# Float32 matmuls for the third batch's projection, and a start whose engine orders are written out as lists, in an attention and feed-forward block of 16 batches

## The chip, the cores and the metric

The kernel runs on 1 core of one Trainium2 chip. The metric is the device time of the whole kernel in microseconds (us), as the median of several runs. Five engines work side by side, each through its own list of instructions in order: PE (TensorE; its weight loads are shown apart as PEld), DVE (VectorE), ACT (ScalarE), POOL (GpSimd) and SP (SyncE, which here only issues DMAs). They wait for one another through semaphores. Matmul results stand in PSUM, eight banks of 128 x 512 float32; everything else stands in SBUF.

## The reference, cut to what matters

`x` is 16 x 512 x 512 (batch, row, column), `ctx` 16 x 512 x 1024. `_layernorm` has no weights.

```python
    def _hnet_depool(h, h_patch_full, patch_lens):
        ...
        _, s = jax.lax.associative_scan(comb, (a_b, u), axis=1)
        depool = s.reshape(bsz, plen, D_MODEL)
        plug = jnp.clip(jnp.cumsum(boundary_mask, axis=1) - 1, 0, plen - 1)
        depool_out = depool[jnp.arange(bsz)[:, None], plug]
        return depool_out + h
    h = rmsnorm(embeds, g_res)
    h = jnp.einsum('bld,ed->ble', h, W_in) + b_in
    h_patch = rmsnorm(patch_embeds, g_init)
    return _hnet_depool(h, h_patch, patch_lens)
...
        r = jax.nn.sigmoid(jnp.einsum('btc,dc->btd', xr, W_r))
        k = jnp.einsum('btc,dc->btd', xk, W_k)
        k_act = jnp.square(jax.nn.relu(k))
        out = r * jnp.einsum('btc,dc->btd', k_act, W_v)
...
    x = x + _L0_xattn_ref(_layernorm(x, axis=-1), ctx_2048, mask_BxS2_if0, ...)
    x = x + _L0_ffn_ref(_layernorm(x, axis=-1), ...)
```

Here `xr` and `xk` mix a row with the row before it (weights `mu_r`, `mu_k`). For each batch there are four products of 512 x 512 by 512 x 512: a (with `W_in`), k, r and v.

## The kernel before

**A batch.** Each batch is cut into four groups j of 128 rows, and the 512 columns into four chunks c. The names in the profile, with their lines:

- `x`: the batch, loaded, later the sum, later the output. Batches 0 to 2 (`BY_PE`, line 420) are transposed by PE into four PSUM banks `tx` (`turn_x`, 629); the others are loaded transposed.
- `split_x` (642): ACT copies each `tx` chunk to a rounded high half `xh[:,0]`, and DVE writes the low half `xh[:,1]` = `tx` - high.
- `wsa` is `W_in` in float32, scaled by `g_res` and less a mean that four float32 matmuls form in the bank `pm` (1112 to 1130); `wha` and `wla` are its halves (`hi_w` 578, `lo_w` 582). The other weights are split likewise: `whk`, `wlk` and so on.
- `a_mm` (786), and `a_first` (799) for batch 0: the projection into the bank `pa`, with three passes for each j (high by high, high by low, low by high; `QW`, 600), each of four matmuls. `a_end` (813) on DVE adds `pa`, times the row's scale `rs`, to `x`, which frees the bank.
- `cx`: the context; ACT squares it, DVE scans it (`scan_u` 733, `scan` 748), with a carry between the rows by PE in the bank `pc`. SP writes the result to DRAM as `dr`; POOL fetches rows of it by index (`gather`, 820; the indices are `plug`) and adds them to `x`.
- `norm2` (827): statistics on DVE, a power on POOL, and `y` on DVE (for batches 0 to 3); PE transposes `y` into four banks `tr` (852). `mix` (864): ACT `prev` and DVE `both` write `pv`, which is split into `m`. Each batch has four mixes for k and four for r.
- k (bank `pk`), r (`pr`) and v (`pw`) are three-pass products like a. The first of batch 0, `k_first` (895), needs four banks.
- `plugs` (1021): counts of boundaries by PE into `cp`; DVE turns them to running marks (`marks`), PE sums those over the rows, and DVE forms the index `plug` (`index`, 1062).

**What sets the order.** Every step is a piece added with `add` (516): the engines that can do it with an estimated cost, what it reads and writes, and a due time. `Plan.order` (119) plays these through and gives each engine its fixed order. Buffers have kinds with few places (`SLOTS`, 308): `ps` and `tr` are four PSUM banks each, `op` are 16 tiles of 128 x 2 x 512. Where `ORDER` names pieces for an engine, that engine takes these in just that order first; before, `ORDER` is empty (437) and due times, shifted by hand for each stage (`SHIFT`, 326), decide. `warm` (585) puts small matmuls ahead of some pieces. All instructions are recorded by one helper, so their line is L300.

Of the kernel before, what the change touches and what calls it, by code (L numbers as in the profile page):

```python
# [11 lines left out]
F32 = mybir.dt.float32  # L12
# [9 lines left out]
P = 128  # L22
T = 512
D = 512
# [265 lines left out]
class InOrder:  # L290
# [25 lines left out]
    "tr": [P, D],  # L316
}
PASS = 0.935
PERIOD = lambda i: (("a", i + 1), ("k", i))
TAT = {3: (0, 1, 2, 3)}  # L320
TAT_OF = {0: {0: (0, 1, 2, 3)}, 1: {0: (0, 1, 2, 3)}, 2: {0: (0, 1, 2, 3)}, 3: {0: (0, 1), 2: (2, 3)}, 4: {0: (0, 1), 2: (2, 3)}}
AHEAD = 20.0
EASE = 1.0
SKIP = 6.0
# [64 lines left out]
    ("sq", 4): 2.2,  # L389
    ("stat1", 4): 2.5,  # L390
    ("store", 4): -10.4,
    ("plugs", 8): -40.0,
    ("plugs", 12): -40.0,
}
ONLY = {
    ("rv", 0): 0,
# [37 lines left out]
KR_DVE_LATE = ()  # L434
NKR = 4
LATE = ()
ORDER = {}
RAW_IN = {2: ("op", "raw")}
CX_IN = {}
NLATE = 4  # L440
NWHOLE = 2
Y_DVE = (0, 1, 2, 3)
LEAD = 12.0
LEAD_LATE = 15.0
NLEAD = 6
# [10 lines left out]
def block_kernel(  # L456
# [77 lines left out]
    def K(name, *parts):  # L534
        return [(name, p) for p in (parts or (0,))]
# [7 lines left out]
    TR = (("tr",), [P, D], F32)  # L543
    HI = ((ACT, 0.52), (DVE, 0.34)) if HI_DVE else ((ACT, 0.52),)
    LO = ((DVE, 0.61), (POOL, 1.26))

    def copy(e, o, i):
        (e.tensor_copy if e is dve else e.copy)(o, i)
# [26 lines left out]
    def st(k, c):  # L575
        return S[f"ws{k}{c // 2}"][:, c % 2]
# [8 lines left out]
    def warm(key, tiles, due):  # L585

        n = WARM.get(key, 0)
        if not n:
            return tiles

        def fn(e):
            for _ in range(n):
                e.matmul(S[next(iter(tiles))][:, :P], ones, ones, start=True, stop=True)

        add((PE, 0.064 * n), fn, (), K(next(iter(tiles))), new=tiles, due=due - 0.064 * n)
        return None
# [32 lines left out]
    def turn_x(b):  # L629
# [3 lines left out]
        for j in J:  # L633
            def fn(e, j=j):
# [4 lines left out]
                [y for n in ns for y in K(n, j)] + ([] if j else K(f"txa{b}")),  # L639
                new=None if j else new, due=when(j))  # L640

    def split_x(b, c):
        if b in BY_PE:
            n, t = f"xh{b}_{c}", f"tx{b}_{c}"
            add((ACT, 0.52), lambda e: e.copy(S[n][:, 0], S[t]), K(t, *J), K(n, 0), new={n: OP}, early=40)
            add((DVE, 0.6), lambda e: e.tensor_tensor(S[n][:, 1], S[t], S[n][:, 0].bitcast(F32), ALU.subtract),
                K(t, *J) + K(n, 0), K(n, 1))
            return
        n, rn = f"xh{b}_{c}", f"raw{b}_{c // 2}"
        add(HI, lambda e: copy(e, S[n][:, 0], S[rn][:, c % 2]), K(rn), K(n, 0), new={n: OP}, early=40)  # L650
        add(LO, lambda e: e.tensor_tensor(S[n][:, 1], S[rn][:, c % 2], S[n][:, 0].bitcast(F32), ALU.subtract),
            K(rn) + K(n, 0), K(n, 1))
# [95 lines left out]
    def scan(b):  # L748
# [23 lines left out]
        for j in J:  # L772
# [10 lines left out]

            add((SP, 0.5), put, K(n), K(f"dr{b}", j), moves=0.73)

    def a_mm(b, j, due, kind=PS):
        n = f"pa{b}_{j}"
        sl = slice(j * P, (j + 1) * P)
        new = warm(("a", b, j), {n: kind}, due)
        for k, (q, w) in enumerate(QW):  # L790
            def fn(e, k=k, q=q, w=w):
                for c in range(NC):
                    e.matmul(S[n], S[f"xh{b}_{c}"][:, q, sl], W2("a", w)[:, c],
                             start=(k == 0 and c == 0), stop=(k == 2 and c == NC - 1))

            add((PE, PASS), fn, [y for c in range(NC) for y in K(f"xh{b}_{c}", q) + K("wla" if w else "wha", c)],
                K(n), new=None if k else new, due=due + k * PASS, early=AHEAD)

    def a_first():

        ns = [f"pa0_{j}" for j in J]
        new = warm(("a", 0, 0), {n: TRP for n in ns}, due["a", 0, 0])
        for k, (q, w) in enumerate(QW):
            for c in range(NC):
                def fn(e, k=k, q=q, w=w, c=c):
                    for j in J:
                        e.matmul(S[ns[j]], S[f"xh0_{c}"][:, q, j * P : (j + 1) * P], W2("a", w)[:, c],
                                 start=(k == 0 and c == 0), stop=(k == 2 and c == NC - 1))

                add((PE, PASS), fn, K(f"xh0_{c}", q) + K("wla" if w else "wha", c), [K(n)[0] for n in ns],  # L810
                    new=new if k == c == 0 else None, due=due["a", 0, 0] + (4 * k + c) * PASS, early=AHEAD)
# [209 lines left out]
    def plugs(b0, n):  # L1021
        cp = f"cp{b0}"
        cnt = lambda: S[cp][:, : n * NJ].rearrange("p (b j) -> p b j", j=NJ)
        pb = lambda: S[cp][:, n * NJ :]
        for b in range(b0, b0 + n):
            oh = f"oh{b}"
            add((DVE, 0.6),
                lambda e, b=b, oh=oh: e.tensor_tensor(
                    S[oh], hj[:, 0, :, b].unsqueeze(2).broadcast_to([P, NC, P]),
                    iota.unsqueeze(1).broadcast_to([P, NC, P]), ALU.is_equal),  # L1030
                K("hj") + K("msk"), K(oh), new={oh: (("tmp",), [P, NC, P], F16)}, early=25, soft=True)

            def count(e, b=b, oh=oh):
                for c in range(NC):
                    e.matmul(cnt()[:, b - b0], S[oh][:, c], ohj[:, c, b], start=(c == 0), stop=(c == NC - 1))

            add((PE, 0.1), count, K(oh) + K("hj") + (K(cp, "a") if b > b0 else []),
                K(cp, b) + ([] if b > b0 else K(cp, "a")),
                new=None if b > b0 else {cp: (("ps", "tr"), [P, n * (NJ + 1)], F32)})

        def marks_1(e):

            bm = S[f"bm{b0}"] = spool.tile([P, 1, NJ], F16, tag="bm", name=f"bm{b0}")
            run = S[f"run{b0}"] = spool.tile([P, 1, NJ], F32, tag="pf", name=f"run{b0}")
            for j in J:
                if j:
                    e.tensor_scalar(run[:, 0, j : j + 1], cnt()[:, 0, j : j + 1], 1.0, run[:, 0, j - 1 : j], ALU.min, ALU.add)
                else:
                    e.tensor_scalar(run[:, 0, 0:1], cnt()[:, 0, 0:1], 1.0, None, ALU.min)
            e.tensor_copy(bm[:, 0, NJ - 1 : NJ], run[:, 0, NJ - 1 : NJ])  # L1050

        def marks(e):
            bm = S[f"bm{b0}"] = spool.tile([P, n, NJ], F16, tag="bm", name=f"bm{b0}")
            e.tensor_scalar(bm, cnt(), 1.0, None, ALU.min)
            for j in range(1, NJ):
                e.tensor_tensor(bm[:, :, j], bm[:, :, j], bm[:, :, j - 1], ALU.add)

        add((DVE, 0.5 if n == 1 else 0.8), marks_1 if n == 1 else marks, K(cp, *range(b0, b0 + n)), K(f"bm{b0}"), soft=n > 1)
        add((PE, 0.05), lambda e: e.matmul(pb(), tri, S[f"bm{b0}"][:, :, NJ - 1], start=True, stop=True),
            K(f"bm{b0}") + K("tri"), K(cp, "p"))  # L1060

        def index(e):
            pf = spool.tile([P, n, NJ], F32, tag="pf", name=f"pf{b0}")
            e.tensor_tensor(pf, S[f"run{b0}" if n == 1 else f"bm{b0}"], pb().unsqueeze(2).broadcast_to([P, n, NJ]), ALU.add)
            e.tensor_scalar(pf, pf, -1.0, 0.0, ALU.add, ALU.max)
            e.tensor_copy(plug[:, b0 : b0 + n], pf)

        add((DVE, 0.6), index, K(cp, "p"), K("plug", *range(b0, b0 + n)), due=INF if b0 else P_DUE, soft=True)


    due, t = {}, T0
# [1 line left out]
    def slot(key, cost=3 * PASS):  # L1073
        nonlocal t
        due[key] = t
        t += cost

    for what, b in START:
        if b < NB and (what != "x" or b in BY_PE):
            for j in J:  # L1080
                slot((what, b, j), 0.43 if what in "tx" else 3 * PASS)
    for i in range(NB):
        n1 = i + 1 < NB
        for what, b in PERIOD(i):
# [10 lines left out]
        due["end", i] = t  # L1095


    add((SP, 0.5), lambda e: e.dma_start(small_in, small_d), (), K("cols") + K("msk") + K("tri"), moves=0.45, at=-9.5)
    load_w("a", at=-9)
    add((SP, 0.5), lambda e: e.dma_start(consts, consts_d), (), K("consts"), moves=0.4, at=-8.5)  # L1100
    for j in J:
        load_x0(j, -8)
    add((DVE, 0.07), lambda e: e.tensor_scalar(om, mu, -1.0, 1.0, ALU.mult, ALU.add), K("cols"), K("om"))

    def heat(e):
# [26 lines left out]
    for c in range(NC):  # L1132
        lo_w("a", c)

    def row(src, dst, k, at):
        add((SP, 0.5), lambda e: e.dma_start(dst, src.unsqueeze(0).broadcast_to([P, D])), (), K(k), moves=0.8, at=at)

    row(ginit[0:D], g_bc, "g_bc", -6.4)
    for j in J:
        load_ctx(0, j, at=-6)  # L1140
    row(brow, b_bc, "b_bc", -5.9)
    at = {k: 0.2 * i - 5 for i, k in enumerate(LOADS)}
    at.update({f"cx1_{j}": at["cx1"] + 0.01 * j for j in J if "cx1" in at})
    if NB > 1:
# [10 lines left out]
    def prepare_batch(b):  # L1155
# [47 lines left out]
            for j in J:  # L1203
                gather(b, j)
        stage = ("a", b)
        if b == 0:
            a_first()
        for j in J:
            if b:
                a_mm(b, j, due["a", b, j], PST if b == 1 else PS)  # L1210
            a_end(b, j)
        if late:
            stage = ("gather", b)
# [122 lines left out]
```

## Time and profile before

| | |
|---|---|
| median of 3 runs | 809.4 us (808.52 to 810.18) |
| the profiled execution, its time | 808.87 us |
| its span, first to last instruction | 807.1 us |
| mean granted TensorE clock | 0.994 |
| PE idle before an instruction, up to 71.5 us | 10.1 us in 10 waits |
| the same from there to the end | 3.7 us in 7 waits |
| projection of batch 0, first matmul | 18.27 us |
| first k matmul (batch 0) | 70.28 us |
| first gather issued by POOL | 36.28 us |
| DVE busy, 10 to 60 us in steps of 10 | 8.77, 9.14, 8.47, 9.39, 9.90 us |
| DMA share, 0 to 30 us in steps of 10 | 0.80, 1.02, 0.72 |

The span is what the profile covers; the time is measured around it and is 1.8 us longer. In the lists of the profile a group has its engine, operation, the tiles it writes and reads (numbers left out), its count and its times. A wait is the idle time of an engine before an instruction, and is put down to what released it last. PEclk is the clock that TensorE was granted, 1.00 being full. One execution is profiled, so all durations come from that one.

### The profile page before, as it was taken

How to read it: one execution, taken by the hardware profiler on the slowest of the kernel's cores; microseconds unless marked ns; L12 is line 12 of the kernel's file. 1: busy time of each engine (PE TensorE's matmuls, PEld its weight loads, DVE VectorE, ACT ScalarE, POOL GpSimd, SP SyncE). 2: the span in 40 equal slices, each digit the busy share in tenths (PEclk: the TensorE clock that was granted, in tenths of full speed). 3: DMA queues.
4: the chain of work that ended last, by engine and by line, in shares of the span. 5: the costliest groups of instructions: out<-in, count | busy, mean ns of one | idle time of the engine just before them, and what ended most of it. 6: DMA issues, size and time to landing. Idle time of an engine off the chain costs nothing. (4 is left out here: it accounts for less than half of the span.)

```text
span 807.1 us, 11158 instructions
## 1 busy us (share of the span) xinstructions
PE 788.4 (98%) x3627; PEld 628.2 (78%) x3627; DVE 594.3 (74%) x1323; ACT 486.0 (60%) x950; POOL 453.1 (56%) x374
## 2 busy tenths in 40 slices
PE   7998999999999999999999999999999999999997
PEld 4776877878787888888788888878788888888885
DVE  6899798989789696785857679685866949464432
ACT  6937496655483767467566756457675664655540
POOL 2843766574767656567665556537856554661220
PEclk8999999999999999999999999999999999999999
DMA  9867586895775777667665766756786674430011
GB/s 327 270 95 262 104 220 170 288 220 160 144 234 147 179 199 206 157 209 145 212 140 171 220 157 209 157 162 152 184 234 157 209 138 171 73 89 0 9 45 52
DMA packets 52554, 134.69 MB, mean 167 GB/s; under 512 B 4752, under 2 KB 5264, under 8 KB 50576
## 3 DMA queue, kind: packets, MB, share of 16 engines
q1 hardware_dynamic: 35744, 102.39, 37.3%
q0 software_dynamic: 16608, 31.46, 24.2%
q8 instruction: 28, 0.46, 0.2%
q14 instruction: 30, 0.25, 0.1%
q10 hardware_dynamic: 144, 0.13, 0.0%
HBM read 85.73 MB, written 33.55 MB: 148 GB/s over the span
## 5 line engine op out<-in xcount | busy, mean ns | idle before, releaser
L300 POOL TENSOR_TENSOR m<-pv,m 128x512 fp32r<-128x512 f32 x86 | 120.9, 1414 | 121.3 <-ACT m L300 59.7
L300 PE MATMUL pa<-wha,xh 128*128 128x512 f32 x512 | 136.7, 404 | 5.8 <-DVE x L300 2.0
L300 PE MATMUL pw<-whv,ka 128*128 128x512 f32 x512 | 139.0, 398 | 0.0
L300 POOL DMA_INDIRECT x<-dr,plug x64 | 113.2, 1769 | 45.3 <-issue 17.0
L300 PE MATMUL pr<-whr,m 128*128 128x512 f32 x512 | 138.4, 397 | 0.0
L300 PE MATMUL pk<-m,whk 128*128 128x512 f32 x512 | 133.8, 396 | 0.6 <-DVE x L300 0.6
L300 ACT ACTIVATE pv<-tr,om 128x384 f32<-128x384 f32 (+1 forms) x256 | 100.8, 485 | 52.4 <-PE tr L300 28.5
L300 DVE SCALAR_TENSOR_TENSOR pv<-tr,small,pv 128x511 f32<-128x511 f32 x128 | 94.9, 741 | 38.7 <-ACT pv L300 37.9
L300 PEld LDWEIGHTS pa<-wha,xh 128*128 128x128 f32 x512 | 96.9, 191 | 31.9 <-DVE x L300 2.8
L300 PEld LDWEIGHTS pk<-m,whk 128*128 128x128 f32 x512 | 95.6, 188 | 24.8 <-DVE x L300 1.0
L300 PEld LDWEIGHTS pr<-whr,m 128*128 128x128 f32 x512 | 95.5, 188 | 23.0 <-DVE kr L300 0.4
L300 PEld LDWEIGHTS pw<-whv,ka 128*128 128x128 f32 x512 | 95.0, 188 | 21.8
L300 ACT CAST m<-pv 128x512 fp32r<-128x512 f32 x128 | 76.1, 642 | 37.1 <-DVE pv L300 31.8
L300 ACT ACTIVATE sg<-pr 128x512 f32<-128x512 f32 x64 | 38.1, 598 | 95.6 <-PE pr L300 88.6
L300 DVE TENSOR_TENSOR ka<-kr,ka 128x512 fp32r<-128x512 f32 x48 | 35.9, 749 | 76.3 <-ACT ka L300 76.2
L300 DVE TENSOR_TENSOR sg<-pw,sg 128x512 f32<-128x512 f32 (+1 forms) x65 | 43.9, 676 | 41.5 <-PE pw L300 41.5
L300 ACT ACTIVATE junk<-cx 128x1024 bf16<-128x1024 f32 x64 | 67.5, 1055 | 6.7 <-DMA cx<-cx 6.1
L300 PE MATMUL pa<-wla,xh 128*128 128x512 f32 x256 | 71.2, 401 | 0.3 <-POOL wla L300 0.3
L300 ACT ACTIVATE y<-x,r 128x512 f32<-128x512 f32 x48 | 38.9, 814 | 53.7 <-DVE r L300 37.4
L300 PE MATMUL pw<-wlv,ka 128*128 128x512 f32 x256 | 70.4, 397 | 0.0
L300 PE MATMUL pr<-wlr,m 128*128 128x512 f32 x256 | 70.3, 396 | 0.0
L300 PE MATMUL pk<-m,wlk 128*128 128x512 f32 x256 | 69.9, 396 | 0.0
(116 smaller groups left out, 1238.9 us busy)
## 6 DMA issues: line engine op xcount, KB each, us to landing
cx<-cx SPq DMA_DIRECT2D x64, 512.0 KB
dr<-cx SPq DMA_DIRECT2D x64, 256.0 KB
out<-x SPq DMA_DIRECT2D x31, 512.0 KB
x<-x SPq DMA_DIRECT2D x15, 1024.0 KB
x<-bc POOLq DMA_DIRECT2D x14, 1024.0 KB
raw<-xT SPq DMA_DIRECT2D x26, 512.0 KB
wsa<-winT SPq DMA_DIRECT2D x2, 512.0 KB
x<-x SPq DMA_DIRECT2D x4, 256.0 KB
```

Source lines behind the costliest of these rows:

```text
L300: r = self._tc.keep_in_program_order(op(*args, **kwargs))
```

## The change

1. **The projection of batch 2 in float32.** With `A_WHOLE = (2,)`, `split_x` no longer splits batch 2. It copies the four `tx` chunks as float32 (`xt`, by ACT or DVE) and `a_mm` does four float32 matmuls for each j, `xt` by `wsa`, in place of twelve on the halves. The unsplit weights `wsa` must stay until then.
2. **Orders as lists.** `ORDER` gives each engine the first part of its order, by piece numbers (in the order of `add`).
3. **Ranks through PSUM.** `plugs` keeps its running sums in float32 for any number of batches, and `index` writes its sum to the bank `cp` and the index from there: two instructions in place of three.
4. **Smaller edits.** The first loads are named in `FIRST`, in the order that they had; the ranks of batches 8 and 12 are shifted 10 earlier; `PST` also for batch 0 in a path that is not used (`ROWS_FIRST` is false).

Pieces of the lists that matter here, as they follow from the order of `add` after the change:

| numbers | piece |
|---|---|
| 0; 1, 2; 3; 4 to 7; 9 to 12 | loads: small; two halves of `wsa`; consts; x0 by j; cx0 by j |
| 17 to 20; 29 to 32 | PE: pm by c; transposes of x0 by j |
| 33, 35, 37, 39; 70 to 73 | ACT: high halves of x0; squares of cx0 |
| 42, 44, 46, 48; 49 to 52 | wha by c; wla by c |
| 89, 215 | PE: carry of batch 0, of batch 1 |
| 120; 121 to 132; 133 to 136 | PE: warm-up; a(0); DVE: its evictions |
| 137 to 140; 143, 146, 149, 152; 153 to 156 | POOL: gathers of batch 0; DVE: y(0); PE: tr(0) |
| 190 to 193; 194 to 201 | PE: transposes of x1; its halves |
| 240 to 255 | a(1): for each j three passes and the eviction (243, 247, 251, 255) |
| 281; 282 to 285; 286 to 289 | PE: warm-up, transposes of x2; its copies |
| 329 to 332, 335 to 338, 340 to 343, 345 to 348 | PE: a(2), one matmul each (334: warm-up) |
| 333, 339, 344, 349 | DVE: evictions of a(2) |
| 371, 375, 379, 383; 415, 419, 423, 427 | DVE: mixes for k; for r (batch 0) |
| 386 to 397; 430 and up | PE: k(0); r(0), v(0) and what follows |

The diff, cut to its core:

```diff
+WHOLE = 0.86
...
-    ("plugs", 8): -40.0,
-    ("plugs", 12): -40.0,
+    ("plugs", 8): -50.0,
+    ("plugs", 12): -50.0,
...
+ORDER = {
+    "tensor": [
+        15, 28, 22, 17, 29, 18, 19, 20, 32, 31, 30, 57, 59, 120, 121, 122, 123, 124, 125, 126, 127,
+        89, 128, 129, 130, 131, 132, 189, 190, 192, 191, 193, 281, 282, 283, 240, 241, 248, 285,
+        242, 284, 244, 249, 245, 250, 329, 330, 246, 334, 335, 331, 153, 336, 252, 154, 156, 155,
+        253, 332, 337, 340, 338, 215, 341, 254, 342, 343, 345, 346, 347, 348, 386, 387, 388, 389,
...
+    "vector": [
+        21, 16, 23, 25, 27, 14, 56, 99, 43, 47, 41, 106, 58, 36, 304, 60, 34, 74, 38, 108, 45, 82,
+        76, 102, 78, 40, 83, 85, 84, 51, 49, 80, 104, 86, 50, 114, 87, 52, 88, 118, 112, 116, 231,
+        110, 225, 92, 90, 94, 96, 318, 233, 228, 133, 135, 134, 316, 136, 234, 197, 237, 238, 195,
+        324, 236, 201, 199, 321, 239, 141, 326, 288, 143, 144, 146, 206, 243, 147, 208, 213, 247,
+        150, 251, 149, 152, 211, 209, 210, 212, 214, 415, 427, 333, 419, 371, 375, 423, 216, 379,
+        255, 383, 218, 222, 220, 344, 339, 349, 61, 417, 421, 63, 65, 425, 429, 67, 172, 174, 69,
...
+    "scalar": [
+        98, 105, 101, 303, 100, 35, 70, 33, 37, 72, 48, 71, 39, 46, 42, 44, 107, 73, 103, 159, 227,
+        157, 224, 230, 323, 163, 317, 161, 202, 229, 226, 196, 232, 320, 200, 194, 198, 319, 322,
+        325, 205, 204, 286, 203, 289, 287, 414, 426, 422, 418, 370, 374, 416, 382, 378, 372, 380,
...
+    "gpsimd": [
+        24, 26, 75, 109, 77, 79, 81, 119, 113, 117, 158, 160, 111, 115, 164, 137, 138, 235, 162,
+        139, 142, 327, 140, 145, 328, 207, 148, 151, 373, 381, 385, 377, 256, 257, 295, 258, 259,
...
+    "sync": [
+        0, 1, 3, 4, 2, 7, 5, 6, 9, 11, 10, 8, 54, 12, 53, 13, 280, 55, 165, 93, 91, 97, 95, 276,
...
+FIRST = ["small", "wa", "consts", "x0", "g", "cx0_0", "cx0_1", "cx0_2", "cx0_3", "b"]
+ROWS_FIRST = False
+A_WHOLE = (2,)
...
     def split_x(b, c):
+        if b in A_WHOLE:
+            if b in BY_PE:
+                n, t = f"xt{b}_{c // 2}", f"tx{b}_{c}"
+                add(CP, lambda e: copy(e, S[n][:, c % 2], S[t]), K(t, *J) + (K(n, "a") if c % 2 else []),
+                    K(n, c % 2) + ([] if c % 2 else K(n, "a")), new=None if c % 2 else {n: STAGE}, early=40)
+            return
...
     def a_mm(b, j, due, kind=PS):
...
+        if b in A_WHOLE:
+            for c in range(NC):
+                add((PE, WHOLE), lambda e, c=c: e.matmul(S[n], xt(b, c)[:, sl], st("a", c), start=(c == 0), stop=(c == NC - 1)),
+                    XT(b, c) + K(f"wsa{c // 2}", c % 2), K(n), new=None if c else new, due=due + c * WHOLE, early=AHEAD)
+            return
...
+            for j in J:
+                if not j:
+                    e.tensor_scalar(run()[:, :, 0], cnt()[:, :, 0], 1.0, None, ALU.min)
...
+                else:
+                    e.scalar_tensor_tensor(run()[:, :, j], cnt()[:, :, j], 1.0, run()[:, :, j - 1], ALU.min, ALU.add)
...
         def index(e):
-            pf = spool.tile([P, n, NJ], F32, tag="pf", name=f"pf{b0}")
-            e.tensor_tensor(pf, S[f"run{b0}" if n == 1 else f"bm{b0}"], pb().unsqueeze(2).broadcast_to([P, n, NJ]), ALU.add)
-            e.tensor_scalar(pf, pf, -1.0, 0.0, ALU.add, ALU.max)
-            e.tensor_copy(plug[:, b0 : b0 + n], pf)
+            e.tensor_tensor(pf(), run(), pb().unsqueeze(2).broadcast_to([P, n, NJ]), ALU.add)
+            e.tensor_scalar(plug[:, b0 : b0 + n], pf(), -1.0, 0.0, ALU.add, ALU.max)
```

## The prediction

> **What bounds the kernel now.** I read the page first, then the PE's waits, then the granted clock in short windows, then the PE and DVE timelines up to the first k matmul.
>
> The page, engines and clock:
> ```profile
> PE 788.4 (98%) x3627; PEld 628.2 (78%) x3627; DVE 594.3 (74%) x1323; ACT 486.0 (60%) x950; POOL 453.1 (56%) x374
> ...
> PEclk8999999999999999999999999999999999999999
> ```
> PE is busy 98% of the span, and the clock is below full only in the first slices. So after the start nothing is worth having but fewer PE passes; elsewhere only PE idle time and lost clock can be won. Where those lie, the list of PE's waits up to 71.5 us says (microseconds in total, times, longest):
> ```profile
> PE pa L300 <- DVE x L300: 2.0, 1, 2.0
> PE cp L300 <- DVE rs L300: 1.9, 1, 1.9
> PE pa L300 <- DVE xh L300: 1.6, 1, 1.6
> PE heat L300 <- DVE hot L300: 1.3, 1, 1.3
> PE pa L300 <- ACT wha L300: 1.2, 1, 1.2
> PE pk L300 <- DVE x L300: 0.6, 1, 0.6
> PE tx L300 <- DVE x L300: 0.5, 1, 0.5
> ```
> With three small ones (0.5, 0.3, 0.2) that makes 10.1 us. The same list from 71.5 us to the end holds only 3.7 us, in pieces of 0.7 and less. The change must therefore win in the first 71 us. One stall costs more than itself, as the windows (length, then PE, PEld, DVE, ACT, POOL busy, PEclk, DMA share, GB/s) show:
> ```profile
> 64.00:66.00 2.00, 0.18 (x1) 0.18 (x2) 2.00 (x6) 2.00 (x5) 2.00 (x2) 1.00 0.96 316
> 66.00:68.00 2.00, 2.00 (x6) 1.57 (x7) 2.00 (x4) 2.00 (x5) 2.00 (x3) 0.57 1.00 378
> 68.00:70.00 2.00, 2.00 (x6) 1.59 (x6) 1.47 (x3) 2.00 (x5) 0.63 (x1) 0.58 1.01 388
> 70.00:72.00 2.00, 1.39 (x6) 0.82 (x6) 1.49 (x3) 2.00 (x4) 0.00 (x0) 1.00 0.87 177
> ```
> PE stood 2.01 us before 65.82, and then ran 66 to 70 at a clock of 0.57 and 0.58: (1-0.57)x2 + (1-0.58)x2 = 1.7 us more. The stop of 1.60 us at 47.45 left the clock at 1.00. While PE stood at 64 to 66, DVE, ACT and POOL were full: DVE did all eight mixes of batch 0 in a row (from 58.76), and the eviction that frees a PSUM bank for the third batch's projection came behind them:
> ```profile
> 64.25 0.74 DVE L300 SCALAR_TENSOR_TENSOR pv<-tr,small,pv 128x511 f32<-128x511 f32 x1
> 64.90 0.21 DVE L300 TENSOR_SCALAR pv<-tr,small 128x1 f32<-128x1 f32 x1
> 65.03 0.74 DVE L300 SCALAR_TENSOR_TENSOR x<-pa,rs,x 128x512 f32<-128x512 f32 x1
> ```
> So the start is PE and DVE in turn; k(0) begins cleanly with the second matmul at 71.28, or 71.05 counted from its first.
>
> **Part 1, the float32 projection of batch 2.** Before: 48 split matmuls. The chain of waits gives a row of 48 the price, and the whole-float32 kind already runs in pm (two records for each of four matmuls; durations min/median/max, first and last start):
> ```profile
> 639.45 11.20 PE pk L300 x48
> ```
> ```profile
> L300 PE MATMUL pm<-wsa,gmean x8: 592/592/646, 5.3 to 8.3; 128*128 128x512 f32 x8
> ```
> Split: 11.20/48 = 0.233, three for each pair of tiles = 0.70. Whole: seven steps in 3.0 us = 0.429 a record, 0.858 a matmul. Sixteen of them are 13.73 us: **+2.53 us on PE**, all of it on the bound engine. Here pm's steps could hold waits: by the durations alone (592 against 396 ns of a split matmul) a record would step at 0.233 x 1.5 = 0.35, which makes 11.2 us and +0; and records that didn't overlap at all, 0.592 each, would make 18.9 us and +7.7. I take pm's step, as its tiles have exactly this shape and type, and keep 0 and, for the far end, half of the way up to +7.7 in the range. The Trainium skill ("FP8 and Floating Point Precision", TensorE Precision Notes) speaks against the change: true FP32 is four passes. At 0.233 each that is an estimate of +3.7 us; pm's row shows two records of 0.429, so 2.53 is used.
>
> What it removes: four DVE subtractions (2.47 us for four, at 37.13) and one of four ACT casts, since one of the four copies out of PSUM now goes to DVE (nearest row, those subtractions: 0.62). SBUF tiles stay equal: two stage tiles hold x, the two of the weights are kept longer. PE no longer waits for a low half in batch 2: the **1.60 us** before 47.45, where DVE was in the middle of those subtractions, goes.
>
> **Part 2, the lists.** I number the pieces in the order in which the code adds them. PE: a(0) as before, transposes of x1, warm-up, half of x2, then a(1), a(2) and tr(0) mixed; behind the last tr(0) (155) stand 253, 332, 337, 340, 338, 215, 341, 254, 342, 343 and 345 to 348: two split passes, eleven whole matmul pieces and the carry, 1.9 + 9.4 + 0.9 = 12.2 us, before k(0) (386). DVE: after y(0,3) (152) five scan steps, then mixes and evictions in turn: 415, 427, **333**, 419, 371, 375, 423, 216, 379, **255**, 383. The eviction that came after eight mixes now comes after two. So the **2.01 us** and the **1.7 us** of clock should go. The 0.50 us at 35.29 (warm-up waiting for a bank) goes too: the first eviction (133) is by then done.
>
> Start-up. SP now issues consts and x0_0 ahead of the second half of the weights, x0_0 lands earlier, that half later; the sum of bytes up to the last of x0 (2.3 MB) is the same, so the transposes of x0 end about 12.3 instead of 11.7, two matmuls of pm (1.7 us) being behind the half. ACT then casts xh and, from the third square on, the weights: four casts of x (0.5 each), three squares (1.05) and four of weights (0.52) end about 19.6, against 20.8. The first a matmul needs the third of these, about 19.1 against 18.27. PE stands more than 2 us again and gets the half clock again, as at 15 to 22. a(0) ends about 33.1 against 32.88: **+0.2**. Bounds -2 (the casts' 1.2 us and a shorter half clock) to +2 (a longer one).
>
> All four wla go to DVE: 3 x 0.62 = 1.85 us more there, on the way to the carry pc(0), which comes about 28 instead of 25.63. Behind it hang dr(0) (four DMAs on SP), the gathers on POOL, the second norm and tr(0). It is covered: the first gather left POOL only at 36.28, behind four wlk (31.11, 4.99 us), 7 us after dr's last issue.
>
> New waits. k0 of a(1) waits for ACT's casts of x1 behind a variance and a sum: about 0.3. tr(0): PE reaches it 20 us after a(0) (split passes 9.3, whole pieces 4.3, transposes, warm-ups 6.2), at about 53.7; y(0,3), at 54.93 before, I put at 54.5 (the gaps between its steps are now filled by others). So 0.8, and **+1.1** with the first. Behind a waiting tr(0) the 12.2 us of PE work are queued.
>
> **Part 3, the rest.** Ranks through PSUM: index falls from three DVE instructions to two (0.17 us), five times; marks of several batches rises from four to five. Nobody near is waiting (the gathers come 20 us later). Earlier ranks of batches 8 and 12, and FIRST (the same order as before): nothing, as PE is the bound there. 0, within 0.3.
>
> **Sum** up to k(0): +2.53 - 1.60 - 2.01 - 1.7 - 0.50 + 0.2 + 1.1 = -1.98; the last bank's wait (0.6) stays, and the smaller idle (0.1) goes: **-2.1 us**.
>
> Cross-check on DVE, busy 65 of 70 us there: -2.47 + 0.62 + 1.85 = 0 work; what it can gain is its idle, 2.5 (for sums on ACT) + 1.0 + 0.4 + 0.3 + 0.2 + 0.2 = 4.6 us. None recovered gives 0, all -4.6, half -2.3. The two sums meet, and I take -2.1. The profiled execution took 808.87 (span 807.1 and 1.8 around it), so 806.8 for its like; its median lay 0.5 higher, so **807.3**.
>
> **The rivals.**
> - *DVE stays the pace* (0.12): it must do the same work, its waits return at other places (the rs power on POOL ahead of y(0,1), ACT's squares), k(0) stays at 71 and the extra PE work fills idle time. 809.4, within 1 us.
> - *A stall at tr(0), slower* (0.23): tr(0) stands in PE's list ahead of 12.2 us of projection that could have run. Each microsecond by which y(0,3) is late is lost in full, and from about 2 us of standing the half clock adds 1.7. The carry's delay (2 us) through dr and the fourth gather could do it, since POOL must issue that behind a power that waits for DVE. Zero gain at 2.1 us late; at 3 us, -2.1 + 3 + 1.7 = +2.6: 812.0. Against it: the 7 us of cover above.
> - *All idle gone* (0.17): 1.60 + 2.01 + 1.7 + 0.5 + 0.6 gone and nothing new: 2.53 - 6.4 = -3.9, 805.5; with half of the 3.7 us of later waits, as the lists reach to about 120 us, 803.6.
>
> **How the numbers follow.** The forecast has 0.48, its own range 805 to 809. Measurement can tell about 0.2%, 1.6 us, so the bound is 807.8. Faster: 0.36 of the forecast's 0.48 and the 0.17; same: the other 0.12 and 0.08 of the DVE rival; slower: the tr(0) rival and 0.04. That is 0.53, 0.20, 0.27. The range runs from 803.4 to 812.0: half of the slow rival lies above it, and little below.
>
> **What would show it.** pa matmuls of batch 2: 32 records at 0.43 steps (right) or otherwise. PE's waits: no "pa from xh" of 1.6 and no "pa from x" of 2.0; a clock of 1.00 from 24 to 80. First k matmul near 69 instead of 70.28. Wrong: a new "tr from y" wait of over 2 us, a second stretch of half clock, or new stalls of over 1 us past 80 us, which I hold to be unchanged.

## The result, and the profile after

The changed kernel takes **813.09 us** (median of 7 runs, 812.02 to 814.44). The kernel before, run beside it, takes 810.12 us (7 runs, 808.52 to 811.35). The ratio is 1.0041, with a 95% interval of 1.0027 to 1.0055: **slower by 3.0 us**. The forecast was 807.3 and faster. The profiled execution of the changed kernel took 813.86 us (span 812.1, mean clock 0.993). It lies 0.8 above its median, and the profiled one of before lies 1.25 below its own. So the spans differ by 5.0 us and the medians by 3.0: about 2 us of what the two traces show is spread between executions, and belongs to no part of the change.

The page of the changed kernel, engines and clock:

```profile
PE 789.8 (97%) x3611; PEld 625.2 (77%) x3611; DVE 595.9 (73%) x1324; ACT 484.8 (60%) x949; POOL 446.9 (55%) x369
...
PEclk8899999999999999999999999999999999999999
```

PE is busy 1.4 us longer than before (789.8 for 788.4), in a span longer by 5.0. So most of what these two traces differ by is idle PE. Its waits up to 71.5 us (total, times, longest, in us):

```profile
PE tx L300 <- DMA x<-x: 2.7, 1, 2.7
PE tr L300 <- DVE x L300: 2.3, 1, 2.3
PE pa L300 <- ACT wha L300: 1.9, 1, 1.9
PE cp L300 <- DVE bm L300: 1.9, 1, 1.9
PE pa L300 <- DVE xh L300: 1.7, 2, 1.3
PE heat L300 <- DVE hot L300: 1.3, 1, 1.3
```

The wait of 2.0 for `x` inside a(2) is down to 0.83 (at 71.61, just past the end of this list). New are 2.3 at `tr(0)`, and two larger waits in the start: 2.7 for x0, which was 0.2, and 1.9 for `wha`, which was 1.2. In PE's timeline (start, duration, instruction, then in brackets the idle time before it and what ended that) the one at `tr(0)` is this:

```profile
55.12 0.38 PE L300 MATMUL tr<-consts,y 128*128 128x128 f32 x2
57.84 0.44 PE L300 MATMUL tr<-consts,y 128*128 128x128 f32 x2 [2.34 <-DVE x L300]
...
71.61 3.70 PE L300 MATMUL pa<-wsa,xt 128*128 128x512 f32 x8 [0.83 <-DVE x L300]
75.59 3.95 PE L300 MATMUL pk<-m,whk 128*128 128x512 f32 x16 [0.28 <-ACT whr L300]
```

After the first two transposes PE stands for 2.34 us; k(0) then starts at 75.59, where it was 70.28 before. What PE waits for is a PSUM bank, which a DVE eviction frees. DVE's timeline says why that was late:

```profile
48.02 0.69 DVE L300 BATCH_NORM_STATS2 sb<-x 128x6 f32<-128x512 f32 x1 [2.52 <-DMA x<-dr,plug]
...
57.04 0.74 DVE L300 SCALAR_TENSOR_TENSOR x<-pa,rs,x 128x512 f32<-128x512 f32 x1
...
59.37 1.00 DVE L300 TENSOR_SCALAR y<-x,r 128x512 f32<-128x512 f32 x2
```

In the kernel before, DVE waited 0.24 us for these rows, and y(0,3) came earlier:

```profile
44.93 0.69 DVE L300 BATCH_NORM_STATS2 sb<-x 128x6 f32<-128x512 f32 x1 [0.24 <-DMA x<-dr,plug]
...
54.39 0.54 DVE L300 TENSOR_SCALAR y<-x,r 128x512 f32<-128x512 f32 x1
```

DVE goes through its list in order. It stood 2.52 us for rows that POOL had fetched by index (the gather of batch 0), and all behind it came late: the eviction at 57.04, and the last of y(0), which ended at 60.4 instead of 54.9. Not all of these 5.5 us are the gather's: in this execution a(0) had already ended 3.1 us later than before.

From 60 to 80 us the clock is now full, where it was 0.57 and 0.58 from 66 to 70 (length, then PE, PEld, DVE, ACT, POOL busy, PEclk, DMA share, GB/s):

```profile
60.00:80.00 20.00, 18.62 (x74) 10.42 (x73) 19.70 (x38) 14.78 (x32) 5.08 (x4) 1.00 0.45 126
```

The float32 matmuls of batch 2 are there, 32 records (min/median/max ns, first and last start):

```profile
L300 PE MATMUL pa<-wsa,xt x32: 590/592/697, 50.3 to 74.7; 128*128 128x512 f32 x32
```

A run of 8 of them takes 3.59 us from the start of the first to the end of the last. Less the last one's 0.59, that is seven steps in 3.00, or 0.429 each, exactly pm's step.

**What differs ahead of the gather.** SP's timeline, after and then before:

```profile
38.42 0.43 SPq L300 DMA_DIRECT2D wsr<-wrT  x1
38.90 0.76 SPq L300 DMA_DIRECT2D wsv<-wvT  x1
39.70 0.47 SPq L300 DMA_DIRECT2D wsr<-wrT  x1
```

```profile
60.44 0.89 SPq L300 DMA_DIRECT2D wsr<-wrT  x2
61.42 0.93 SPq L300 DMA_DIRECT2D wsv<-wvT  x2
```

Three loads of 512 KB, weights of r and v, are now issued at 38.4 to 39.7 instead of 60.4 to 61.9 (the fourth stays late, at 70.58). They stand in the new list of SP, behind batch 1's context, in a line of it that the cut diff above leaves out:

```python
    "sync": [
...
        167, 168, 166, 170, 179, 169, 217, 180, 219, 221, 223, 277, 278, 470, 279, 475, 474, 468,
```

(170 and 169 are the halves of `wsr`, 179 and 180 those of `wsv`.) POOL issues the four gathers of batch 0 from 38.8 to 50.9, right beside them.

### The profile page after: what moved, and what is told of

It reads as the page before. It is cut to its first block, busy times and chain, and to the rows that moved or that the text cites. A ratio compares the mean times of both kernels' runs of the same rounds, so it can differ in the third digit from the quotient of the medians.

```text
span 812.1 us, 11089 instructions
## 1 busy us (share of the span) xinstructions
PE 789.8 (97%) x3611; PEld 625.2 (77%) x3611; DVE 595.9 (73%) x1324; ACT 484.8 (60%) x949; POOL 446.9 (55%) x369
## 4 chain that ended last, share of the span: by engine, by line
PE 70%; DVE 12%; DMA 9%; POOL 3%; issue 3%; ACT 2%; SPq 0%; DVEq 0%; POOLq 0%; ACTq 0%
PE pr L300 17%; PE pw L300 17%; PE pk L300 16%; PE pa L300 15%; DVE cx L300 3%; DMA cx<-cx 3%; PE tr L300 3%; DVE pv L300 3%; DMA dr<-cx 2%; DMA x<-dr,plug 2%; POOL x L300 1%; DVE x L300 1%; DVE sg L300 1%; DMA x<-bc 1%; ACT junk L300 1%
## 5 line engine op out<-in xcount | busy, mean ns | idle before, releaser
L300 POOL TENSOR_TENSOR m<-pv,m 128x512 fp32r<-128x512 f32 x85 | 117.1, 1388 | 105.5 <-ACT m L300 49.7
L300 POOL DMA_INDIRECT x<-dr,plug x64 | 115.0, 1796 | 50.3 <-DMA x<-bc 19.9
L300 PE MATMUL pa<-wha,xh 128*128 128x512 f32 x480 | 128.9, 404 | 4.1 <-ACT wha L300 1.9
L300 PEld LDWEIGHTS pa<-wha,xh 128*128 128x128 f32 x480 | 90.8, 191 | 28.9 <-issue 2.7
L300 ACT CAST m<-pv 128x512 fp32r<-128x512 f32 x128 | 76.8, 645 | 40.3 <-DVE pv L300 39.7
L300 DVE TENSOR_TENSOR ka<-kr,ka 128x512 fp32r<-128x512 f32 x53 | 39.9, 752 | 80.9 <-ACT ka L300 80.8
L300 POOL TENSOR_TENSOR r<-r,mhalf 128x1 f32<-128x1 f32 x64 | 38.6, 606 | 59.1 <-DVE r L300 47.7
```

What stands on the lines that cost most here:

```text
L300: r = self._tc.keep_in_program_order(op(*args, **kwargs))
```

## The experiments

Each run was timed against the kernel before on the same chip, in 5 rounds; the medians are in us, the ratios with their 95% intervals. The runs were spread over three chips, so runs on different chips are compared by their ratios. One execution of each was profiled; for the float32 part alone, the start put back and the kernel before with loads moved forward it was the slowest of that kernel's runs (about 3 us above the median), and with both repairs it was 2.5 above; their traces show more loss than the medians do. "First gathers" below is the median time from issue to landing of batch 0's four gathers.

**Each part by itself.** The first question was which part loses. My theory was then the start: in the profiled execution x0 came late (the wait of 2.7), and a(0) ended 3.1 us later than before. The rival was the DVE list.

*The float32 projection alone*, on the kernel before, with the orders from due times as before:

```diff
+A_WHOLE = (2,)
```

> The kernel before with the float32 projection of batch 2 and nothing else; orders come from due times again. Theory 1 (the lists' start and loads cost the time): +2.5 us on PE less the 1.6 us wait for a low half of x2, so about +1, 811 (809.5 to 812). Theory 2 (the result, +3.0 us, is just the +2.53 us of the 16 float32 matmuls, and all the rest cancels): +2.5 to +3, 812.6 to 813.1. 32 records of the float32 matmuls, 0.43 us apart, under both.

817.2, ratio 1.0090 [1.0070, 1.0109], far above both expectations. k(0) starts at 70.06, no later than before, so the matmuls aren't paid for there. PE's waits from 68 to 160 us show where the loss is:

```profile
PE tr L300 <- DVE y L300: 3.9, 3, 3.2
PE pk L300 <- DVE cx L300: 1.8, 1, 1.8
```

The planner had laid out all that follows in another way, and its order stalls for y of a later batch (3.2 us at 137.32). So this run prices the planner's new order, and not the matmuls alone.

*All lists, batch 2 split again* (`A_WHOLE` empty, the lists renumbered; the four subtractions go back to DVE):

```diff
-A_WHOLE = (2,)
+A_WHOLE = ()
```

> The changed kernel with batch 2 split again (12 split passes in the list in place of the 16 float32 matmuls, four subtractions on DVE behind the second statistics of batch 0). Theory 1: the first a matmul stays at about 22 us in place of 18.3, the gathers still land beside the weights of r and v, so it stays slower than before: +1 to +4, 811 to 814. Theory 2: without the 2.53 us it comes back to before, 810.1 within 0.7.

811.71, ratio 1.0027 [1.0015, 1.0039]. Slower without the float32 matmuls too, so the lists hold a loss of their own.

*The changed kernel with the old order of the first loads and of PE's first pieces:*

```diff
-        15, 28, 22, 17, 29, 18, 19, 20, 32, 31, 30, 57, ...
+        15, 22, 28, 17, 18, 19, 20, 29, 30, 31, 32, 57, ...
...
-        0, 1, 3, 4, 2, 7, 5, 6, 9, 11, 10, 8, 54, 12, 53, 13, 280, 55, 165, 93, 91, 97, 95, 276,
+        0, 1, 2, 3, 4, 5, 6, 7, 8, 9, 10, 11, 12, 13, 53, 54, 55, 280, 165, 93, 91, 97, 95, 276,
```

> The changed kernel with the first 18 loads on SP and the first 11 pieces on PE put back to the order of before (both halves of the weights, then consts and x0; four pm matmuls, then the transposes). Theory 1: pm ends near 9 us, x0's transposes near 11.7, the first a matmul comes at 18.3 to 19.1 instead of 21.96, a(0) ends 2.5 to 3 us earlier, and the time falls by 2 to 3, to 810 to 811. Theory 2: the start is covered, 813 within 0.7.

813.95, ratio 1.0056 [1.0039, 1.0072]. Nothing is won back. Here a(0) waited 2.54 us for `wha` and began at 20.89; ACT's list, which casts `wha`, was still the new one.

*The changed kernel with no lists* (`ORDER = {}`):

> The changed kernel with an empty table of orders: float32 projection and the new ranks, orders from due times. Theory 1: like the float32 projection alone, 811 (809.5 to 812.5), with the first a matmul near 18.3. Theory 2: 812.6 to 813.1.

817.88, ratio 1.0098 [1.0083, 1.0112]: the same as the float32 part alone, within the intervals. With float32 in place the lists are therefore worth 0.57%, some 4.6 us, against the planner's order. This is not their worth against the order before.

**The start, the loads and the matmuls, one at a time.** Four runs on one chip.

*The float32 matmuls in the exact order of before* (each of PE, DVE, ACT and POOL is given the order that it had before, as a list):

```diff
+A_WHOLE = (2,)
+ORDER = {
...
+}
```

> The kernel before with the float32 projection of batch 2, and with every other instruction of PE, DVE, ACT and POOL kept in the order that before has (written out as lists; SP by due times, four lines apart). Theory 1 (float32 alone is cheap; the +7.6 us of the version by due times came from the orders that due times then chose): +2.5 us on PE less the 1.6 us stop for a low half, +0 to +2.5 in all. Theory 2 (float32 is dear by itself, by the buffers that it holds or by its passes): +5 or more.

812.3, ratio 1.0024 [1.0011, 1.0037]: +2.1 us between the medians. That is the net price of the float32 part where nothing is rearranged. The sum's terms for it were +2.53 and -1.60, the wait before x2's low halves, which goes here too; so +2.1 is no confirmation of +2.53. Nor is it paid ahead of k(0), which starts at 70.59 in this trace: from there to the end the kernel takes 739.4 us, and before, from 71.05, 736.1. Why it is lost behind k(0) wasn't followed up. The run also shows that the +7.6 of the float32 part alone came with the planner's other order.

*The weights of r and v held until piece 335*, a float32 matmul of PE, and nothing else changed:

```diff
+HOLD = 335
...
+    for n in (169, 170, 179, 180):
+        plan.pieces[n].before.add(HOLD)
+        plan.pieces[HOLD].after.add(n)
```

> The changed kernel, with the loads of the weights of r and v (four pieces on SP) held until PE has done the first matmul of the second tile of a(2), about 53 us, instead of going out at 38. Theory 1 (these loads slow the gathers of batch 0): gathers land 5 to 6 us after their issue instead of 9.2, y(0,3) ends 3 us earlier, the wait before tr(0) shrinks from 2.3 to under 1, time -1.5 to -3, 810 to 811.5. Theory 2 (the gathers wait for something else): landing at 9 us still, 813 within 0.8.

**810.37, ratio 1.0001 [0.9989, 1.0012]**: the whole loss has gone. SP's and PE's timelines of this kernel:

```profile
51.11 0.38 SPq L300 DMA_DIRECT2D wsr<-wrT  x1
```

```profile
52.32 0.44 PE L300 MATMUL tr<-consts,y 128*128 128x128 f32 x2 [0.16 <-DVE x L300]
...
70.06 3.96 PE L300 MATMUL pk<-m,whk 128*128 128x512 f32 x16 [0.28 <-ACT whr L300]
```

The loads leave at 51.11, the stop at `tr(0)` is 0.16 instead of 2.34, and k(0) starts at 70.06 instead of 75.59. DVE no longer waits for a gather at all. Of these 5.5 us, 3.35 are not the loads': they stand already at the first matmul of a(1). In the changed kernel's execution x0's transposes began later (9.38 against 7.83), and the clock was 0.50 from 20 to 26, where here it is 1.00 from 20 to 40. Changed first, then with the loads held:

```profile
41.90 1.17 PE L300 MATMUL pa<-wha,xh 128*128 128x512 f32 x4 [1.29 <-DVE xh L300]
```

```profile
38.55 1.17 PE L300 MATMUL pa<-wha,xh 128*128 128x512 f32 x4 [1.30 <-DVE xh L300]
```

The other 2.2 us are those of the stop.

*The start put back* (loads and PE as above, and ACT's casts of `wha` in the order 42, 44, 46, 48):

> The changed kernel with the old order of the first loads and first PE pieces, and with ACT's four casts of the a weights in the order of their use (c 0, 1, 2, 3 in the places that held 3, 2, 0, 1). Theory 1 (a(0) waits for the third cast): first a matmul at 18.2 to 18.8 instead of 20.89 with the old loads alone and 21.96 as changed; -1.5 to -3 against the changed kernel. Theory 2 (the middle is paced by DVE, so the start is given back): k(0) within 0.7 of the 73.8 that the old loads alone have.

813.31, ratio 1.0037 [1.0024, 1.0051]: no gain. a(0) began at 18.43, but then stood 1.89 us for `rs` from DVE (at 26.70) and ran at a clock of 0.50 and 0.71 from 28 to 32, and it ended at 35.8, as in the changed kernel (35.9). The time won at the head of a(0) was given back further on. The theory of the start falls.

*Both, the start put back and the loads held:*

> Both repairs, of the start and of the loads of r and v. Theory 1: the two gains add, k(0) near 70, time 808.5 to 810. Theory 2: no better than one of them, 811 to 813.

811.46, ratio 1.0012 [0.9999, 1.0026]: the two repairs don't add. Against the run with the start alone, on the same chip, holding the loads gives 1.9 us.

**The loads, from the other side.** If they are the cause, they must also hurt the kernel before.

*The kernel before, in its own exact order, with three of the loads moved forward* (only SP's order differs):

```diff
+HOLD = 281
...
+    for n in (169, 170, 179):
+        p = plan.pieces[n]
+        p.at, p.early = 27.0, INF
+        p.before.add(HOLD)
+        plan.pieces[HOLD].after.add(n)
```

> The kernel before, every instruction of PE, DVE, ACT and POOL in its order, with three of the four loads of the weights of r and v moved on SP from 60 us to behind the second batch's context, about 36 us, where the changed kernel has them. Theory 1 (these loads slow the gathers, and that is what the changed kernel lost): gathers land 8 to 9 us after issue instead of 5 to 6.6, y(0,3) ends 2 to 4 us later than 54.9, and the time rises by 2 to 4, to 812 to 814. Theory 2 (before has room for it, and the lists lose by their own order): within 1 of before.

**817.45, ratio 1.0085 [1.0066, 1.0103]**: +7.4 us from three transfers that left at 60 us before, about twice what was expected. Timelines of SP, DVE and PE:

```profile
38.07 0.38 SPq L300 DMA_DIRECT2D wsv<-wvT  x1
38.49 0.98 SPq L300 DMA_DIRECT2D wsr<-wrT  x2
```

```profile
48.17 0.69 DVE L300 BATCH_NORM_STATS2 sb<-x 128x6 f32<-128x512 f32 x1 [2.44 <-DMA x<-dr,plug]
```

```profile
50.38 2.08 PE L300 MATMUL pa<-wha,xh 128*128 128x512 f32 x4 [3.12 <-DVE xh L300]
```

It is the same wait of DVE for a gather (2.44 us), and PE then stands 3.12 us. At that place the kernel before has the 1.60 us that the prediction counts:

```profile
47.45 1.20 PE L300 MATMUL pa<-wha,xh 128*128 128x512 f32 x4 [1.60 <-DVE xh L300]
```

The longer stop costs clock as well, and a second one comes late; two windows of this kernel, from two queries:

```profile
50.00:54.00 4.00, 3.62 (x10) 2.92 (x11) 3.93 (x13) 0.00 (x0) 3.21 (x4) 0.58 0.89 155
...
130.00:150.00 20.00, 17.01 (x72) 13.03 (x71) 16.12 (x36) 9.96 (x25) 12.52 (x11) 0.91 0.52 132
```

The clock is 0.58 from 50 to 54. From 130 to 150 PE is busy 17.01 us where it was 19.82 in the kernel before: `tr` waits 0.90 and 2.00 us there for y of a later batch. k(0) was 4.1 us late (74.36), of which 0.8 is a later x0; the rest of the loss was added behind it. How the one led to the other wasn't followed up, and this trace is 3.2 us above its kernel's median.

*The loads held, and batch 2 split again* (`A_WHOLE = ()`, with the lists renumbered and `HOLD = 338`, which keeps the loads until 52.1):

> The changed kernel with the late loads of r's and v's weights and with batch 2 split again (twelve split passes in the list). Theory 1 (the float32 matmuls cost their 2.5 us on PE here too, less what they free on DVE): 1 to 2 us under the late loads alone, 808.5 to 809.5, a little under before. Theory 2 (in this order DVE is the bound and the four subtractions cost as much as the matmuls): 810.4 within 0.7.

810.06, ratio 1.0000 [0.9989, 1.0011]. This equals the run with the loads held and float32 (1.0001): in the list order float32 costs nothing that can be measured. I had expected to see its price there. The two traces end alike (808.3 and 808.2) though k(0) starts at 72.79 here and at 70.06 there, so what float32 wins ahead of k(0) is lost behind it. And here PE stands at `tr(0)` with the loads held just as it did without (early loads first):

```profile
56.76 0.44 PE L300 MATMUL tr<-consts,y 128*128 128x128 f32 x2 [1.81 <-DVE x L300]
```

```profile
55.04 0.44 PE L300 MATMUL tr<-consts,y 128*128 128x128 f32 x2 [1.83 <-DVE x L300]
```

DVE's wait for a gather went all the same (2.5 us with the early loads, none here), and from the first matmul of a(1) to k(0) PE took 33.8 us instead of 34.7.

*The loads held longer*, to piece 253 (`HOLD = 253`; they leave at 57.50):

> The changed kernel with the loads of r's and v's weights held still longer, until the second pass of the last tile of a(1), about 57 us, behind all four gathers. Theory 1: the last gathers land a little sooner, 0 to -1 against the late loads (810.4). Rival: the weights come too late for ACT's casts of r's weights, +1 or more, with waits of PE for whr or wlr.

810.76, ratio 1.0006 [0.9994, 1.0018]. Holding them past 51 us wins nothing more.

*The ranks through PSUM alone*, with the two shifts of -50, on the kernel before:

> The kernel before with only the new ranks (through PSUM, two instructions in the index in place of three) and the shift of -50 for batches 8 and 12. Both theories: no change, 810.2 within 0.8; a rival for the rest of the loss would be +1 or more here.

809.91, ratio 1.0000 [0.9983, 1.0017]: nothing, as forecast.

## Why the prediction was wrong

**The cause.** In the profiled executions the time from issue to landing of the first gathers sorts by one thing, when the three loads leave (the trace of the kernel before has no landing times for them):

| kernels | three loads leave at | first gathers, us (median of 4) |
|---|---|---|
| changed; old loads and PE; start put back; lists without float32 | 36 to 40 | 8.4; 8.1; 8.3; 8.3 |
| before with loads moved forward | 38 | 6.4 |
| loads held (four kernels) | 51 to 58 | 5.2 in each |
| changed with no lists | 59 | 5.4 |
| before's order with float32; ranks alone; float32 alone | 59 to 62 | 4.8; 4.8; 5.1 |

The gathers as the traces of the changed kernel and of the one with the loads held have them (durations on POOL, first and last start; then issue to landing):

```profile
L300 POOL DMA_INDIRECT x<-dr,plug x4: 1629/1719/1876, 38.8 to 50.9; - x4
...
DMA to landing us min/median/max: 4.5/8.4/9.7
```

```profile
L300 POOL DMA_INDIRECT x<-dr,plug x4: 1573/1680/1877, 35.6 to 45.4; - x4
...
DMA to landing us min/median/max: 4.6/5.2/5.6
```

POOL spends as long on each (1.72 and 1.68 us); the transfer takes 3.2 us longer. The windows from 42 to 50 show what it shares the DMA engines with, after and then with the loads held:

```profile
42.00:46.00 4.00, 4.00 (x20) 3.29 (x21) 3.50 (x5) 2.19 (x6) 3.84 (x4) 1.00 0.96 283
46.00:50.00 4.00, 4.00 (x21) 3.28 (x20) 1.91 (x9) 3.97 (x9) 1.77 (x3) 1.00 1.09 292
```

```profile
42.00:46.00 4.00, 4.00 (x21) 3.26 (x20) 3.48 (x13) 3.94 (x9) 3.82 (x4) 1.00 0.37 65
46.00:50.00 4.00, 4.00 (x20) 2.49 (x19) 2.24 (x8) 0.93 (x2) 4.00 (x4) 1.00 0.64 96
```

The DMA engines are full (0.96, 1.09) instead of at 0.37 and 0.64. So the chain in the changed kernel is: loads beside gathers, gather late, DVE stands in order, eviction and y(0) late, PE stands at `tr(0)`, k(0) late. That the loads cost the time, and that they do it through late gathers and a waiting DVE, is shown from both sides, by taking the loads away and by adding them to the kernel before. Where PE then stands depends on the order: at `tr(0)` in the changed kernel, before x2's halves in the kernel before with the loads moved forward. With the lists and batch 2 split, `tr(0)` stands 1.8 us with and without the early loads, so the late gather is not the only thing that can stop PE there. The Trainium skill ("DMA: Bandwidth & Descriptors", Queues, rings and completion order) says that each DMA engine takes turns between the queues it has work for, packet by packet. The later landings agree with that in direction; no run here shows the turns themselves.

**Size.** Holding the loads was worth 0.40% (1.0041 against 1.0001), 0.27% without float32 (1.0027 against 1.0000) and 1.9 us with the start put back: 1.9 to 3.2 us, against a loss of 3.0. (Only the last pair is known to have run on one chip; in the others each run was timed against the kernel before.) The 1.1 us between the changed kernel and its lists without float32 lie within their intervals.

**By the prediction's own steps:**

- *"+2.53 us on PE"* for float32. The step of 0.429 was exact. In a frozen order the float32 part cost 2.1 net; in the list order it cost nothing measurable once the loads were held. That it fills idle time there is likely, but not shown.
- *"-1.60", "-2.01", "-1.7 of clock", "-0.50"*. The 1.60 us before x2's halves, the 0.50 at 35.29 and the half clock at 66 to 70 went, as forecast; of the 2.01 us behind the mixes 0.83 is left. (That the clock is below full "only in the first slices" was read off the page too strictly: its 9 means 0.90 or more, and hid these four microseconds.) And a wait of 1.29 us for x1's halves is new (at 41.90), where the sum had 0.3, so that the 1.60 was mostly moved and not won.
- *"Start-up ... +0.2".* Nothing speaks against it: with the loads held a(0) ended at 32.6 (33.1 forecast), and two kernels with the old start, 1.0056 and 1.0037, weren't better than the changed one at 1.0041. The late x0 was this one execution's: with the same first loads four other profiled executions began the x0 transposes at 7.08, 7.15, 7.83 and 8.33 us, this one at 9.38, and a(0) at 19.0 to 19.5, this one at 21.96. I had said 19.1.
- *"It is covered: the first gather left POOL only at 36.28 ... 7 us after dr's last issue."* **Here it failed.** The issue was covered (35.6 with the loads held); the landing was not. I counted the time up to a gather's issue and let it land as before, without asking what else SP's list now put into the DMA engines at that time. I had followed that list for the first loads only, so the early weights of r and v stood in the sum at nothing, without a reason. They cost 1.9 to 3.2 us.
- *"y(0,3) ... I put at 54.5. So 0.8."* It ended at 60.4, some 3.3 us of it from this execution's late start and 2.2 from the gather, and `tr(0)` stood 2.34 us. With the loads held, y(0,3) ended at 54.8 and `tr(0)` stood 0.16. So 54.5 was a good estimate; the late gather was missing from it. But the 0.8 doesn't follow from its own terms: 33.1 for the end of a(0), 0.3 of waiting and the listed 9.3, 4.3 and 6.2 make 53.2 and not 53.7 for PE at `tr(0)`, so the wait should have been 1.3.
- *The rival "a stall at tr(0), slower", 812.0.* It had the place and nearly the price (813.1 measured), but another mechanism: the carry, or POOL's power ahead of the fourth gather. That the price came so near is luck: 1.7 of it was half clock, and in the changed kernel's trace the clock stayed at 1.00 behind this stop. The kernel before with the loads moved forward stalls with gathers issued as early relative to its start as before, so that mechanism isn't needed. I held the "7 us of cover" against this rival, and that was the wrong cover.
- *The sum, -2.1.* Even with the loads held the change is at 1.0001, within 0.12%. Its profiled k(0) starts at 70.06, so 1.0 us was won up to there, not 2.1: of the idle time on which the sum counted, 1.3 us for x1's halves and 0.83 for an eviction in a(2) came back.
- *"New stalls of over 1 us past 80 us, which I hold to be unchanged."* **Here it failed a second time.** PE has a new wait past 80 us, in the changed kernel this one:

```profile
96.51 1.20 PE L300 MATMUL pw<-whv,ka 128*128 128x512 f32 x4 [1.21 <-ACT sg L300]
```

All eight kernels with the new lists have it (1.14 to 1.21 us; with the loads held it is 1.20, at 91.20); the kernel before has no wait over 0.7 us there. No run took that wait away, so what it costs in the end stays open: from k(0) to the end the changed kernel takes 736.5 us in its trace, the one with the loads held 738.1, and the kernel before 736.1 (from 71.05). So the 1.0 us won ahead of k(0) with the loads held is lost again behind it.

- *The rival "DVE stays the pace" (809.4, no change)* has the number that fits once the loads are held. That DVE sets the pace isn't shown by it.

**What stays open.** Why the planner's order, once batch 2 is float32, stalls at 72 and at 137 us is shown only to be a matter of order, and not which piece does it. Why time won up to k(0) doesn't reach the end is open too. Which of the three loads hurts most, and whether another queue would have spared the gathers, wasn't tried.

## What to carry to other kernels

When a list or a planner moves a load, look at what is in flight at its new time, above all small transfers that an engine in order waits for; a load isn't free because nobody needs it yet. Price a transfer up to its landing, under the traffic of its new place, and not up to its issue. And price one part of a change with everything else frozen in its order: the same matmuls came with 7.6 us when the planner was free to rearrange and with 2.1 when it wasn't. Follow the change to the end of the kernel as well: time won in one stretch can be lost in the next.

## What the runs showed of the hardware that was not expected

- **A row gather beside bulk loads.** Four gathers of 128 rows, 256 KB each, landed in a median of 4.8 to 5.4 us without the three loads (eight kernels), and in 8.1 to 8.4 us (longest 9.1 to 9.7) beside them, in the four kernels with lists that load early; in the kernel before with the loads moved forward it was 6.4 (longest 9.0).
- **The clock after a stop.** The stop of 2.34 us at `tr(0)` left the clock at 1.00 in the changed kernel; one of 2.33 us at the same place, in the kernel with the start put back, was followed by 0.62 and 0.53 (58 to 62 us), and 3.12 us in the kernel before with early loads by 0.58. Stops of 2.01 us (the kernel before, 0.57) and 2.02 us (old loads, 1.00) differ in the same way. So a stop of about 2 us may or may not cost clock; the 1.7 us that I added "from about 2 us" is not certain.
- **When x0's transposes can begin** differs by 2.3 us between profiled executions with the same first loads (7.08 to 9.38). One trace of such a start is no measure of it.
